# Which engine issues which transfer: patch writes on GpSimd's queue, maxima on SyncE between the patch loads

## The chip, the cores and the metric

One core of one Trainium2 chip runs the whole kernel. The metric is the time of one execution in device microseconds (us). Most executions of one kernel agree within 0.3%; all runs compared here are undisturbed (fast) ones. Five engines run in parallel, each with its own in-order queue: TensorE (PE; its weight loads are PEld), VectorE (DVE), ScalarE (ACT), GpSimd (POOL) and SyncE (SP), which only issues transfers here.

## The reference

Each of two layers replaces a 3x3 convolution by a soft lookup. Every channel's nine-pixel patch is compared with 16 centroids, a softmax over the 16 distances makes weights, and the weights pick from a table.

```python
def amm_conv3x3(x, centroids, w_sub, stride=1):          # x: (16, 256, 28, 28), centroids: (256, 16, 9)
    patches = conv_general_dilated_patches(x, (3, 3), (stride, stride), 'SAME')
    p = patches.reshape(B, C, s, Ho * Wo).transpose(0, 3, 1, 2)
    d = sum(p * p)[..., None] - 2.0 * einsum('bncs,cks->bnck', p, centroids) + sum(centroids * centroids)
    attn = softmax(-d, axis=-1)
    lut = einsum('cks,cso->cko', centroids, w_sub)
    out = einsum('bnck,cko->bno', attn, lut)
    return out.transpose(0, 2, 1).reshape(B, -1, Ho, Wo)
# per image: group norm -> amm (layer 0) -> batch norm, relu -> amm (layer 1) -> batch norm
#            -> squeeze-excite gate -> relu(. + its input) -> + x
```

## The kernel before

The work is cut into 32 stages (16 images, two layers), and each stage into 16 slots of 5 to 7 us (two tiles of 384 and 400 pixels, 8 groups of channels each). Stages of the two layers alternate. In a slot TensorE multiplies patches with centroids (the logits, L563), ScalarE exponentiates (L621), TensorE multiplies the exponentials with the centroids (the numerators, L631), VectorE transposes these (nt, L643) and takes reciprocals (rc, L649), GpSimd scales (k, L659, and small sums, L671), VectorE transposes back (q) and TensorE accumulates outputs (L695).

Three kinds of transfer feed this. **Patch writes** (L468): the image and two shifted copies of it are written to a patch buffer in device memory, 12 writes for an image and layer, during the stage before it is used. **Patch loads** (L550): SyncE reads four pieces of that buffer for each slot, three slots ahead. **Maxima**: for two of the eight groups of channels of layer 1 the largest logit is found six slots ahead, and is moved to the rows of the patch tile by way of device memory: `mt` (VectorE) to `dm` (L602), then `dm` to `pt` (L608).

```python
def to_pat(l, i, pat, px=0, n=HW):                     # patch write; L468 is the issue
    dx, k, h = STEPS[i]
    ...
    nc.scalar.dma_start(view(pat, ...), bass.AP(v.tensor, ...))      # [cut]

def patches(u, tile):                                  # patch loads of one slot
    ...
    for i in range(4):
        nc.sync.dma_start(pt[32 * i : 32 * i + ROWS, :, :n], view(u["pat"], ...))   # L550 [cut]

def m_turn(u):                                         # VectorE, L595
    mt = small.tile([P, 4, 32], F32, name="mt")
    nc.vector.transpose(mt..., u["mx"]...)             # [cut]

def m_out(u):
    d = drot.tile([4 * 256, 32], F32, tag="dm", name="dm")
    for p0, n in ((0, P), (P, 96)):
        nc.scalar.dma_start(view(d, ...), u["mt"][:n])               # L602 [cut]
    u["dm"] = d

def m_in(u):
    for j in range(NCH):
        nc.scalar.dma_start(u["pt"][MROW + j :: 32, :, :n], view(u["dm"], ...))     # L608 [cut]

# the order of work within one slot
LOGITS, EXP, LOOK_A, NUM, TURN, SMALL, LOOK_B, MAX, LOOK_C, TURN_BACK, LOAD, REST = range(12)
...
    a = s - self.lb                                    # six slots ahead
    at(a, MAX, a_logits, u)
    ...
    at(a + 2, TURN_BACK, m_turn, u)
    at(a + 3, TURN, m_out, u)
    at(a + 4, TURN, m_in, u)
```

## Time and profile before

| | before |
|---|---|
| time, median of 2 (range) | 3105.42 us (3103.16 to 3107.68) |
| span of the profiled run, mean granted clock | 3103.0 us, 0.972 |
| TensorE busy, idle | 2966.8 us (96%), 136 us |
| the 13 layer-0 stages between 396 and 2711 us, mean | 96.7 us |
| the layer-1 stages (14), mean | 88.3 us |
| first logits, first numerators start | 45.7 us, 54.8 us |

The stage times are the distances between the first numerator matmuls of successive stages in the timeline. Time at half clock counts as busy, so the 136 us of idle time aren't all that can be won.

The lines themselves are in the prediction below. A waits line such as `SPq L550 <- DMA pat<-side: 650.6, 180, 14.0` reads: instructions of line 550 on SyncE's queue were held until a transfer pat<-side landed, 650.6 us in total, 180 times, at most 14.0 us. The `q` marks the queue, which for SyncE is all there is.

### The profile page before, as it was taken

How to read it: one execution, taken by the hardware profiler on the slowest of the kernel's cores; microseconds unless marked ns; L12 is line 12 of the kernel's file. 1: busy time of each engine (PE TensorE's matmuls, PEld its weight loads, DVE VectorE, ACT ScalarE, POOL GpSimd, SP SyncE). 2: the span in 40 equal slices, each digit the busy share in tenths (PEclk: the TensorE clock that was granted, in tenths of full speed). 3: DMA queues.
4: the chain of work that ended last, by engine and by line, in shares of the span. 5: the costliest groups of instructions: out<-in, count | busy, mean ns of one | idle time of the engine just before them, and what ended most of it. 6: DMA issues, size and time to landing. Idle time of an engine off the chain costs nothing.

```text
span 3103.0 us, 94273 instructions
## 1 busy us (share of the span) xinstructions
PE 2966.8 (96%) x39834; PEld 1165.8 (38%) x39834; DVE 2254.3 (73%) x2760; ACT 1094.8 (35%) x1605; POOL 1506.4 (49%) x2163
## 2 busy tenths in 40 slices
PE   4998999999999999999999999999999999999997
PEld 3432333333333333333333333333333433334333
DVE  3464777777777777777777787777777777777785
ACT  2331342433434233342433334243343423333332
POOL 2352454555545455464545545455453545546444
PEclk8998999999999999999999999999999999999998
DMA  7866777767757676675767767676775767664552
GB/s 204 215 148 133 202 201 188 190 163 190 187 148 188 148 202 169 182 183 146 192 158 199 182 165 184 157 194 156 192 187 144 193 148 202 171 170 114 146 136 58
DMA packets 339391, 530.25 MB, mean 171 GB/s; under 512 B 94240, under 2 KB 265488, under 8 KB 338960
## 3 DMA queue, kind: packets, MB, share of 16 engines
q10 hardware_dynamic: 151488, 244.45, 31.5%
q1 hardware_dynamic: 180560, 241.14, 30.6%
q0 software_dynamic: 6912, 38.54, 4.2%
q8 instruction: 316, 5.18, 0.7%
q14 instruction: 115, 0.94, 0.1%
HBM read 269.96 MB, written 254.05 MB: 169 GB/s over the span
## 4 chain that ended last, share of the span: by engine, by line
PE 76%; DMA 10%; DVE 5%; POOL 3%; issue 2%; ACT 2%; ACTq 1%; SPq 0%; POOLq 0%; DVEq 0%
PE acc L695 45%; PE pair L631 15%; PE pair L563 15%; DMA pt<-pat 6%; DMA pat<-side 3%; DVE nt L643 2%; POOL k L659 1%; DVE rc L649 1%; ACT e L621 1%; DVE q L677 1%; POOL total L671 1%; DMA pat<-im 1%; ACTq L468 1%; PE pair L324 1%; DVE gn_st L417 0%
## 5 line engine op out<-in xcount | busy, mean ns | idle before, releaser
L695 PE MATMUL acc<-q,ws 128*128 128x384 f32 (+1 forms) x4096 | 1662.5, 525 | 5.3 <-ACT y L717 5.3
L659 POOL TENSOR_TENSOR k<-nt,rc 128x832 f32<-128x832 f32 (+1 forms) x512 | 804.8, 1572 | 1538.5 <-DVE rc L649 1527.1
L643 DVE STREAM_TRANSPOSE nt<-pair 128x832 f32<-128x832 f32 (+1 forms) x1024 | 977.4, 993 | 765.3 <-PE pair L631 640.7
L621 ACT ACTIVATE e<-pair 128x800 f32<-128x800 f32 (+1 forms) x1024 | 787.3, 821 | 1499.7 <-PE pair L563 1308.7
L695 PEld LDWEIGHTS acc<-q,ws 128*128 128x128 f32 x4096 | 705.1, 191 | 922.5 <-issue 610.0
L563 PE MATMUL pair<-pt,wd 19*32 19x384 f32 (+2 forms) x18432 | 626.5, 509 | 60.5 <-DMA pt<-pat 58.6
L631 PE MATMUL pair<-e,cw 32*32 32x384 f32 (+1 forms) x16384 | 585.9, 507 | 14.5 <-ACT e L621 13.3
L677 DVE STREAM_TRANSPOSE q<-k 128x832 f32<-128x832 f32 (+1 forms) x512 | 489.2, 956 | 0.8 <-POOL k L659 0.8
L649 DVE RECIPROCAL rc<-nt 128x104 f32<-128x104 f32 (+1 forms) x512 | 398.6, 779 | 17.6
L563 PEld LDWEIGHTS pair<-pt,wd 19*32 19x32 f32 (+1 forms) x18432 | 149.3, 103 | 440.6 <-issue 265.6
L631 PEld LDWEIGHTS pair<-e,cw 32*32 32x32 f32 x16384 | 167.2, 104 | 360.5 <-ACT e L621 317.9
L665 POOL TENSOR_TENSOR tail<-nt,rc 128x104 f32<-128x104 f32 (+1 forms) x512 | 245.1, 479 | 0.0
L695 PE MATMUL acc<-qt,ws 128*128 128x400 f32 (+1 forms) x512 | 218.8, 509 | 0.0
L671 POOL TENSOR_TENSOR total<-total,nt 128x96 f32<-128x96 f32 (+1 forms) x448 | 200.3, 447 | 0.0
L671 POOL TENSOR_TENSOR total<-total,rc 128x96 f32<-128x96 f32 (+1 forms) x448 | 179.1, 400 | 0.0
L695 PEld LDWEIGHTS acc<-qt,ws 128*128 128x128 f32 x512 | 91.0, 190 | 100.8 <-issue 51.3
L587 DVE TENSOR_REDUCE mx<-z 128x48 f32<-128x768 f32 (+1 forms) x128 | 120.8, 944 | 0.0
L582 DVE STREAM_TRANSPOSE z<-pair 128x768 f32<-128x768 f32 (+1 forms) x128 | 119.4, 971 | 1.8 <-PE pair L563 1.8
L707 ACT ACTIVATE im<-acc,bnsh,bnsc 128x384 f32<-128x384 f32 (+1 forms) x64 | 43.4, 678 | 137.0 <-PE acc L695 135.2
L717 ACT ACTIVATE y<-acc,bnsh,bnsc 128x384 f32<-128x384 f32 (+1 forms) x64 | 43.4, 679 | 88.7 <-PE acc L695 79.5
L525 DVE SCALAR_TENSOR_TENSOR y<-xt,gn_rstd,y 128x392 f32<-128x392 f32 x64 | 71.2, 1116 | 1.2 <-ACT y L519 1.2
L533 POOL TENSOR_TENSOR y<-y,xt 128x392 f32<-128x392 f32 x64 | 64.8, 1015 | 11.0 <-ACT y L529 11.0
(104 smaller groups left out, 620.7 us busy)
## 6 DMA issues: line engine op xcount, KB each, us to landing
pat<-side ACTq DMA_DIRECT2D x232, 588.0 KB
pt<-pat SPq DMA_DIRECT2D x1024, 112.5 KB
pt<-pat SPq DMA_DIRECT2D x1024, 108.0 KB
pat<-im ACTq DMA_DIRECT2D x116, 588.0 KB
xt<-in_x POOLq DMA_DIRECT2D x32, 784.0 KB, 8.7
out_dram<-y POOLq DMA_DIRECT2D x16, 784.0 KB, 6.4
pat<-side ACTq DMA_DIRECT2D x24, 300.0 KB
pat<-side ACTq DMA_DIRECT2D x24, 288.0 KB
```

The lines of the kernel that those rows point to most:

```text
L563: nc.tensor.matmul(ps[t // 2][c : c + 32, t % 2, :n], lhsT=wd[l][32 * i : 32 * i + rows, 4 * u["m"] + t, :], rhs=u["pt"][32 * i : 32 * i + ...
L582: nc.vector.transpose(z[:, : 64 * nb].rearrange("p (t m) -> p t m", t=2), ps[:, :, : 32 * nb])
L587: nc.vector.tensor_reduce(u["mx"][:, 2 * v : 2 * v + 2].rearrange("p t (j b) -> p t b j", j=2)[:, :, :nb], u["z"].pop(0)[:, : 64 * nb].rea ...
L621: nc.scalar.activation(e[:, :, :n], ps[:, :, :n], AF.Exp, scale=2.0)
L631: nc.tensor.matmul(u["nm"][t // 2][32 * i : 32 * i + 32, t % 2, :n], lhsT=cw[l][c : c + 32, 4 * u["m"] + t, :], rhs=es[t // 2][c : c + 32, ...
L643: nc.vector.transpose(nt[:, :nb, 2 * v : 2 * v + 2].rearrange("p b t r -> p t b r"), ps[:, :, : 32 * nb].rearrange("p t (b r) -> p t b r", ...
L649: nc.vector.reciprocal(rc[:, : 8 * nb], u["nt"][:, :, SUM])
L659: nc.gpsimd.tensor_tensor(q[:, :nb].rearrange("p b (a s) -> p (b a) s", s=8), nt[:, :, :8], rc.unsqueeze(2).to_broadcast([P, 8 * nb, 8]), ...
L665: nc.gpsimd.tensor_tensor(tails[key][:, :nb, 8 * (m % 4) : 8 * (m % 4) + 8], nt[:, :, 8].rearrange("p (b a) -> p b a", a=8), rc.rearrange( ...
L671: nc.gpsimd.tensor_add(t[:, : 8 * nb], t[:, : 8 * nb], v)
L677: nc.vector.transpose(q[:, :, : 32 * nb].rearrange("p h (b r) -> p h b r", r=32), u.pop("k")[:, :nb].rearrange("p b (h r) -> p h b r", h=2),)
L695: nc.tensor.matmul(accs[key][:, :n], lhsT=ws[l][:, 2 * m + h if h < 2 else 2 * NQ + m // 4, o * P : (o + 1) * P], rhs=u["q"][h][:, :n], st ...
```

## The change

The intent: ScalarE, which has exponentials to do, loses both kinds of transfer that it issues all through the run. The patch writes go to GpSimd, the maxima to SyncE, and in a slot SyncE's loads and then the maxima now come right behind the logits.

```diff
@@ to_pat
-        nc.scalar.dma_start(
+        nc.gpsimd.dma_start(
@@ m_out
-            nc.scalar.dma_start(view(d, 32 * p0, ...), u["mt"][:n])
+            nc.sync.dma_start(view(d, 32 * p0, ...), u["mt"][:n])
@@ m_in
-            nc.scalar.dma_start(
+            nc.sync.dma_start(
@@ the order within a slot
-    LOGITS, EXP, LOOK_A, NUM, TURN, SMALL, LOOK_B, MAX, LOOK_C, TURN_BACK, LOAD, REST = range(12)
+    LOGITS, LOAD, MOVE, EXP, LOOK_A, NUM, TURN, SMALL, LOOK_B, MAX, LOOK_C, TURN_BACK, REST = range(13)
-                        at(a + 3, TURN, m_out, u)
-                        at(a + 4, TURN, m_in, u)
+                        at(a + 3, MOVE, m_out, u)
+                        at(a + 4, MOVE, m_in, u)
```

## The prediction

> **What bounds the kernel now.** I read the page first (busy shares, then clock), then TensorE's waits, then SyncE's own waits, then the stretches around one stall. The first two parts of the page:
>
> ```profile
> PE 2966.8 (96%) x39834; PEld 1165.8 (38%) x39834; DVE 2254.3 (73%) x2760; ACT 1094.8 (35%) x1605; POOL 1506.4 (49%) x2163
> ...
> PEclk8998999999999999999999999999999999999998
> DMA  7866777767757676675767767676775767664552
> ```
>
> (The DMA row is the 40 slices' busy share.) TensorE is busy 96% of 3103 us and nothing else comes near, so only its idle time and its slow time can be won. The idle time is 136 us; TensorE's waits say what ends it (us in total, times, longest):
>
> ```profile
> PE pair L563 <- DMA pt<-pat: 58.6, 39, 4.9
> PE pair L423 <- DVE gn_mv L418: 14.9, 2, 12.3
> PE pair L631 <- ACT e L621: 13.3, 23, 4.5
> ```
>
> The largest is matmuls waiting for the patch loads (SyncE's pt<-pat); only 13.3 us wait for ScalarE. So why are loads late, with a lead of three slots (512 slots, 6 us each)? SyncE's own waits over the run:
>
> ```profile
> SPq L550 <- DMA pat<-side: 650.6, 180, 14.0
> SPq L550 <- DMA pat<-im: 404.4, 63, 15.1
> SPq L550 <- DMA pt<-pat: 378.1, 491, 4.6
> SPq L550 <- DMA dm<-mt: 304.6, 55, 21.4
> ```
>
> The patch loads wait 1360 us for transfers that ScalarE issues (patch writes pat<-side and pat<-im, maxima dm<-mt). Nearly all of it isn't data: the patch buffers were written a stage earlier. The built program gives the DMAs of SyncE and ScalarE together eight completion semaphores, taken in turn in program order, and each DMA waits for the earlier one on its semaphore. So a load waits for the write eight DMAs before it, and that write waits in ScalarE's queue behind exponentials and behind the wait for dm to land. One such place in stretches (us; busy time of PE, PEld, DVE, ACT, POOL; clock; DMA share; GB/s):
>
> ```profile
> 1020.00:1034.00 14.00, 14.00 (x183) 5.14 (x182) 11.92 (x16) 3.13 (x4) 7.72 (x11) 1.00 0.74 195
> 1034.00:1039.00 5.00, 1.43 (x4) 0.31 (x4) 1.74 (x2) 0.00 (x0) 2.00 (x4) 0.96 0.80 214
> 1039.00:1045.00 6.00, 6.00 (x40) 1.67 (x41) 0.00 (x0) 1.56 (x2) 0.00 (x0) 0.50 0.62 139
> ```
>
> From 1025.2 to 1033.5 us SyncE waits once, 8.3 us, for a pat<-side that ScalarE issued at 1025.90. ScalarE's timeline there:
>
> ```profile
> 1024.78 1.08 ACTq L602 DMA_DIRECT2D dm<-mt  x2
> 1025.90 0.61 ACTq L468 DMA_DIRECT2D pat<-side  x1
> ...
> 1032.11 1.17 ACTq L608 DMA_DIRECT2D pt<-dm  x2
> ```
>
> The load misses its slot, TensorE stands 3.6 us, and then runs 6 us at clock 0.50: the stall costs twice. What it costs in all is seen from equal stretches, each with the 512 numerator matmuls of one stage (16 slots):
>
> ```profile
> 952.40:1049.90 97.50, 93.25 (x1245) 35.75 (x1244) 69.06 (x82) 37.04 (x56) 51.04 (x77) 0.96 0.71 177
> 2711.20:2798.80 87.60, 87.60 (x1235) 34.50 (x1234) 68.13 (x81) 30.43 (x43) 41.21 (x58) 1.00 0.64 164
> 2798.80:2885.50 86.70, 86.70 (x1244) 34.55 (x1243) 69.24 (x82) 32.37 (x49) 49.55 (x70) 1.00 0.48 113
> ```
>
> The first is a layer-0 stage with the stall, the second a layer-1 stage, the third a layer-0 stage with no patch writes beside it and no stall. Cutting the timeline the same way, the 13 layer-0 stages between 396 and 2711 us take 93.8 to 98.5 us, mean 96.7; the layer-1 stages 87.5 to 90.5.
>
> **What the Trainium skill says.** (1) "DMA: Bandwidth & Descriptors", section "Issuing engines are not separate DMA queues": all issuers' transfers interleave on the same 16 engines, and another issuer saves only sequencer time. The trace agrees on the engines (share 0.74 with both queues active), so I expect no bandwidth from the move; but it doesn't speak of the coupling through shared semaphores that I found above. (2) "TensorE: Matmul & The Clock Gate", Part 1, "What's actually happening": an idle window of some 3.4 us brings the clock to half, a busy one restores it. The trace agrees: 0.50 for 6 us after the 5 us hole. (3) "Perfetto Trace Analysis", section "DMA Instruction — SWDGE (GPSIMD)": what is recorded of a GpSimd DMA is descriptor generation by its cores, up to the last core. So I take the recorded 756 ns (out<-y) and 812 ns (xt<-in) medians as time taken from GpSimd. (4) "SBUF — State Buffer", "SBUF: two separate sides": a VectorE operation in a two-port mode keeps GpSimd from writing descriptors. No sign of it here: the 32 xt issues took 747 to 872 ns beside a VectorE busy 73%.
>
> **The change part by part.**
> ScalarE loses 420 patch writes of about 0.60 us (582 to 610 median), 128 dm of 0.45 and 128 pt<-dm of 0.567: 252 + 58 + 73 = 383 us of its sequencer, and the 118.4 us that it stood before an exponential until dm had landed. Beside TensorE's work almost all of that was hidden: worth 10 us of the 13.3 at most.
> GpSimd gains 420 issues of about 0.78 us (my choice between 756 and 812): 328 us, 1506 + 328 = 1834 us, 59%. In a slot: k 1.57, tail 0.48, totals 0.85 make 2.9 us, plus 0.78 is 3.7 of 6 us. It still has room. VectorE's nt waits 103 us already for GpSimd's totals (two nt buffers), all catching up after stalls, so a GpSimd that is late by a slot would be felt.
> SyncE gains 256 issues of about 0.5 us, 128 us, and 64 waits for dm to land (7.3 us in the timeline above: 1024.78 to 1032.11). It has loads three slots ahead, 18 us, so 7 us fits.
> The coupling goes: in the changed program the hardware semaphores belong to SyncE alone and GpSimd's DMAs use the eight software ones. Loads wait for real data or earlier loads.
> Gains: 13 stages x (96.7 - 87.6) = 118 us, of which I take 90%, 106; the layer-1 stages' small stalls, 10 us in all, half: 5; the near stall at 2926.8 us, 6; the stretch from 180 to 305 us, which takes 126 us where a clean stage takes 88 and where loads and weight moves on SyncE wait for patch writes: 10 of 38, as true dependences stay there.
> Losses: at the start GpSimd now issues 12 patch writes before sq (L389, at 16.4 us before). 12 x 0.78 = 9.4 us, and writes 9 to 12 wait for the semaphores of 1 to 4; sq moves to about 27 us, and with it VectorE's sorting, which releases TensorE at 33.5 us. Part was slack behind loads: 9 us lost. Where patch writes are close before their loads (image 0 and image 15 of layer 1), GpSimd's turn in a slot comes some 6 us after ScalarE's, since scaling waits for numerators and VectorE: 3 us.
> Sum: 106 + 5 + 6 + 10 - 9 - 3 = 115 us; 3105 - 115 = 2990.
>
> **Rivals.**
> A, GpSimd becomes the gate: its in-order queue stands at a patch write (waiting for a semaphore or for side), scaling is late, nt buffers aren't free, TensorE's ring fills. For: 103 us of such waits now, and in slots 0 to 3 there are four writes each. Against: 59% load. If each stage lost 3 us by it: 32 x 3 = 96, hence about 3085, the same.
> B, the wait moves: SyncE stands for dm to land and the loads behind it are late. For: longest wait on dm 21.4 us. Against: that was ScalarE's queue; now dm goes out when the maxima are ready, with three slots before use. Half the gain lost would be 3045.
> C, loads were late from DMA contention. For: share 0.80 in the hole. Against: SyncE issued nothing for 8.3 us before it, and the stretch before has 0.74 at full speed. If C, 3090.
> D, everything goes, also 38 us of the start: 2950.
>
> **Range and chances.** I weigh: main line 70%, A or B in part 20%, C or worse 10%. **2990 us**, range 2950 to 3060. Faster by over 2% means under 3043: 0.82; within 2%: 0.15; slower: 0.03.
>
> **What would show it.** Right: SyncE's waits name no pat<-side except at a stage's first load; PE waiting for pt<-pat falls from 58.6 to under 20 us; layer-0 stages take 87 to 89 us; clock dips between 300 and 2700 us vanish; GpSimd's pat issues take 0.7 to 0.9 us; first logits come near 54 us instead of 45.7. Wrong: issues over 1.2 us, or VectorE's nt waiting for GpSimd in hundreds of us (A); pt<-pat waits released by dm landings (B); holes with loads issued in time (C).

## More of the kernel before

The program names no completion semaphores. Whoever builds it hands them out to the transfers and adds the waits.

## The result, and the profile after

The changed kernel takes **2973.64 us** (median of 2, 2970.91 to 2976.36), the kernel before 3105.42. The ratio is 0.9576, with a 95% interval of 0.9527 to 0.9624. A ratio here is always the mean time of one kernel's fast runs over the mean time of the other's fast runs of the same rounds, so it isn't quite the ratio of the medians quoted.

The page of the kernel after, busy time, granted clock and DMA share:

```profile
PE 2871.6 (97%) x39834; PEld 1145.4 (39%) x39834; DVE 2252.7 (76%) x2760; ACT 1092.7 (37%) x1605; POOL 1768.5 (60%) x2583
...
PEclk8999999999999999999999999999999999999998
...
DMA  6877777767767676776767667676776767674641
```

TensorE executes the same 39834 matmuls in 95.2 us less busy time. Its idle time falls from 136 to 98 us. So 38 us of the gain are in the holes themselves, and more is in what follows them: summed over the trace, the time lost to halved clock (the missing share of the clock times its duration) is 88.4 us before and 32.2 us after, 56 us less. The rest of the 95 us isn't taken apart. All 12 dips between 300 and 2700 us are gone. The DMA row hardly moves, so there is no sign that the transfers became cheaper.

TensorE's waits after (total us, times, longest):

```profile
PE pair L423 <- DVE gn_mv L418: 20.6, 14, 12.3
PE pair L396 <- POOL sq L389: 12.9, 1, 12.9
PE pair L631 <- ACT e L621: 10.6, 20, 6.4
PE acc L695 <- ACT y L717: 9.7, 1, 9.7
...
PE pair L563 <- DMA pt<-pat: 3.3, 7, 0.7
```

The wait that led the list before, logits for patch loads, fell from 58.6 us to 3.3. Three lines have grown: the wait for `sq` at the start (3.0 us before), the many short waits for group-norm statistics (`gn_mv`, 14.9 before) and one wait near the end for the last layer's output `y` (5.3 before). All are looked at below. SyncE's own waits after:

```profile
SPq L550 <- PE pair L563: 580.6, 361, 5.7
SPq L602 <- DVE mt L595: 547.5, 62, 15.2
SPq L550 <- DMA pt<-pat: 245.4, 327, 3.0
...
SPq L550 <- DMA pat<-side: 59.0, 10, 9.9
```

The loads now wait mostly for TensorE to release a patch buffer, which is the wait that one wants, or for earlier loads. Waits for patch writes fell from 1055 us (pat<-side and pat<-im) to 59. Note the second line: SyncE stands 547.5 us until VectorE has the maxima ready, up to 15.2 us at a time, and yet loads arrive in time, because three slots are more than 15 us.

Two successive stages of the kernel after, layer 0 and then layer 1 (us; busy time of PE, PEld, DVE, ACT, POOL; clock; DMA share; GB/s):

```profile
1254.00:1342.30 88.30, 87.71 (x1248) 34.63 (x1248) 69.31 (x82) 37.08 (x56) 59.25 (x89) 1.00 0.72 187
1342.30:1430.10 87.80, 87.45 (x1237) 34.65 (x1236) 70.57 (x87) 30.46 (x44) 49.23 (x71) 1.00 0.68 180
```

A layer-0 stage takes 88.3 us at full clock where the one shown in the prediction took 97.5 at 0.96. Slot by slot, most of that is in the fifteenth slot: 14.8 us on average in the thirteen layer-0 stages before, 7.46 in each of them after.

Where the time went, from the starts of the stages in both traces (us, negative is a gain):

| part | before | after | difference | predicted |
|---|---|---|---|---|
| first numerators start | 54.8 | 60.8 | +6.0 | +9 |
| first stage | 124.9 | 117.0 | -7.9 | 0 |
| second stage (from 180 us) | 125.8 | 103.6 | -22.2 | -10 |
| 13 layer-0 stages | 1257.8 | 1149.2 | -108.6 | -106 |
| 14 layer-1 stages | 1235.4 | 1235.6 | +0.2 | -5 |
| stage from 2799 us | 86.7 | 86.4 | -0.3 | 0 |
| stage from 2886 us | 97.9 | 89.1 | -8.8 | -6 + 3 |
| last stage and end | 119.6 | 127.5 | +7.9 | 0 |
| span | 3103.0 | 2969.2 | -133.8 | -115 |

### The profile page after: what moved, and what is told of

The parts are those of the page before. It is cut to its first block, busy times and chain, and to the rows that moved or that the text cites. A ratio compares the mean times of both kernels' runs of the same rounds, so it can differ in the third digit from the quotient of the medians.

```text
span 2969.2 us, 94838 instructions
## 1 busy us (share of the span) xinstructions
PE 2871.6 (97%) x39834; PEld 1145.4 (39%) x39834; DVE 2252.7 (76%) x2760; ACT 1092.7 (37%) x1605; POOL 1768.5 (60%) x2583
## 4 chain that ended last, share of the span: by engine, by line
PE 79%; DMA 7%; DVE 6%; POOL 4%; issue 2%; ACT 2%; SPq 0%; ACTq 0%; DVEq 0%; POOLq 0%
PE acc L695 47%; PE pair L631 16%; PE pair L563 14%; DMA xt<-in_x 4%; DVE nt L643 2%; POOL k L659 2%; DVE rc L649 1%; DVE gn_st L417 1%; POOL total L671 1%; DMA pt<-pat 1%; ACT e L621 1%; DMA ws<-dws 1%; PE pair L309 0%; PE pair L324 0%; DVE q L677 0%
## 5 line engine op out<-in xcount | busy, mean ns | idle before, releaser
L695 PE MATMUL acc<-q,ws 128*128 128x384 f32 (+1 forms) x4096 | 1641.0, 519 | 9.7 <-ACT y L717 9.7
L695 PEld LDWEIGHTS acc<-q,ws 128*128 128x128 f32 x4096 | 696.9, 189 | 907.7 <-issue 577.2
L631 PE MATMUL pair<-e,cw 32*32 32x384 f32 (+1 forms) x16384 | 580.3, 502 | 11.9 <-ACT e L621 10.6
L563 PE MATMUL pair<-pt,wd 19*32 19x384 f32 (+2 forms) x18432 | 561.0, 500 | 5.9 <-DMA pt<-pat 3.3
L563 PEld LDWEIGHTS pair<-pt,wd 19*32 19x32 f32 (+1 forms) x18432 | 138.4, 103 | 340.1 <-issue 265.5
L468 POOL DMA_DIRECT2D pat<-side x280 | 186.6, 667 | 1.1 <-DMA pat<-im 0.7
L468 POOL DMA_DIRECT2D pat<-im x140 | 94.0, 672 | 3.5 <-ACT im L447 3.5
```

The costliest lines, as they stand in the source:

```text
L468: nc.gpsimd.dma_start(view(pat, (ROWS * p0 + 9 * k + 3 * dx) * HW + px, [[ROWS * HW, m], [HW, 3], [1, n]]), bass.AP(v.tensor, v.offset, [l ...
L563: nc.tensor.matmul(ps[t // 2][c : c + 32, t % 2, :n], lhsT=wd[l][32 * i : 32 * i + rows, 4 * u["m"] + t, :], rhs=u["pt"][32 * i : 32 * i + ...
L631: nc.tensor.matmul(u["nm"][t // 2][32 * i : 32 * i + 32, t % 2, :n], lhsT=cw[l][c : c + 32, 4 * u["m"] + t, :], rhs=es[t // 2][c : c + 32, ...
L695: nc.tensor.matmul(accs[key][:, :n], lhsT=ws[l][:, 2 * m + h if h < 2 else 2 * NQ + m // 4, o * P : (o + 1) * P], rhs=u["q"][h][:, :n], st ...
```

## The experiments

Twelve kernels were run, each in three rounds against the kernel before on the same chip, whose median there lay between 3107 and 3110 us. All gave correct results. Where an edit adds lines, line numbers in that kernel's trace are up to two higher.

| run | kernel | median us (range) | ratio to before [95%] |
|---|---|---|---|
| e1_pat_only | before + only patch writes to GpSimd | 3110.73 (3107.61 to 3111.84) | 1.0013 [0.9992, 1.0035] |
| e2_max_only | before + only maxima to SyncE, with the new order | 3033.74 (3024.67 to 3035.87) | 0.9757 [0.9730, 0.9783] |
| e3_order_only | before + loads early in the slot (built the same program, see below) | 3109.40 (3104.28 to 3114.92) | 1.0014 [0.9991, 1.0037] |
| e10_old_order | after, in the old order | 2974.66 (2970.66 to 2978.24) | 0.9568 [0.9537, 0.9599] |
| e4_ticks | after + tiny unrelated transfers on ScalarE | 3035.80 (3030.02 to 3043.10) | 0.9765 [0.9739, 0.9790] |
| e9_max_on_act | after, maxima back on ScalarE | 3330.48 (3328.10 to 3335.38) | 1.0715 [1.0682, 1.0748] |
| e7_pool_busy | after + more work on GpSimd | 2984.57 (2984.05 to 2986.70) | 0.9599 [0.9570, 0.9628] |
| e11_all_gpsimd | before, patch writes and maxima to GpSimd, old order | 3147.74 (3144.10 to 3155.68) | 1.0121 [1.0096, 1.0145] |
| e12_gpsimd_early | after, maxima on GpSimd, new order | 2973.85 (2972.79 to 2979.95) | 0.9572 [0.9547, 0.9597] |
| e5_sq_first | after + squares ahead of the first writes | 2964.37 (2962.18 to 2967.47) | 0.9536 [0.9507, 0.9565] |
| e6_xt_early | after + input images one slot earlier | 2963.25 (2962.48 to 2965.42) | 0.9524 [0.9508, 0.9540] |
| e8_best | after + four repairs | 2942.73 (2937.89 to 2947.80) | 0.9465 [0.9447, 0.9482] |

**The theory**: transfers of SyncE and of ScalarE share eight completion semaphores, and one that reuses a semaphore waits for the transfer that used it before. Loads were late because they stood behind ScalarE's issues in this way, and the change ends it by leaving ScalarE without regular issues. **The rivals**: the place in the slot (new order) does it; the load on the DMA engines does it; or GpSimd's or SyncE's new issues cost what was won.

### e1: the patch writes alone

```diff
@@ before, to_pat
-        nc.scalar.dma_start(
+        nc.gpsimd.dma_start(
```

> Only the patch writes go to GpSimd; the moves of the maxima stay with ScalarE and the order of the slot is as before. Theory (loads are late because they share completion semaphores with ScalarE's patch writes): nearly all of the gain, 2975 to 3005 us; SyncE's loads wait no more for pat, only for dm and pt<-dm; layer-0 stages 88 to 90 us. Rival 1 (the maxima, through ScalarE's wait for dm to land, make the loads late): 3050 us or more. Rival 2 (both parts are needed): some 3030 to 3060.

Measured: 3110.73 us, no gain at all. The theory's 2975 to 3005 us failed, because it took the waits for the maxima to be harmless. The first rival's 3050 us or more came true, but e2 below will speak against the maxima as the only cause. SyncE's waits, then TensorE's, over the whole run:

```profile
SPq L550 <- DMA dm<-mt: 837.3, 80, 24.0
...
SPq L550 <- DMA pat<-side: 57.4, 13, 12.4
```

```profile
PE pair L563 <- DMA pt<-pat: 43.0, 42, 3.4
```

The loads no longer wait for patch writes (57.4 us), but they wait 837.3 us for the maxima instead, up to 24.0 us, and TensorE still waits 43.0 us for them. The two layer-0 stages from 1132 and 1318 us take 96.2 and 96.8 us, with the fifteenth slot at 15.5 and 15.8. One such place: between 1000 and 1032 us SyncE's queue has

```profile
SPq L550 <- DMA dm<-mt: 24.6, 2, 23.0
```

and ScalarE's timeline of the same kernel has the issues that it waits for:

```profile
1016.36 1.56 ACT L621 ACTIVATE e<-pair 128x800 f32<-128x800 f32 x2 [3.50 <-PE pair L563]
1019.15 1.92 ACTq L602 DMA_DIRECT2D dm<-mt  x2
...
1025.78 2.54 ACTq L608 DMA_DIRECT2D pt<-dm  x2
```

The first dm goes out at 1019.15, as soon as VectorE has the maxima ready (1019.12), and lands at 1023.75. The load is issued at 1023.81, after 23.0 us of waiting for it, which is more than the 18 us of three slots. A load of patches has no use for maxima. In the trace the load waits on the very semaphore that this dm counts, and then counts on it itself.

The semaphore numbers, which the trace keeps for every transfer, show the same over the whole run. Of the 1360 us that loads wait for ScalarE's transfers in the kernel before, 1339 are waits on the semaphore that the load itself uses next; so are all 837.3 us here. The 2835 transfers of the two queues before make one strict turn through eight semaphores (354 or 355 transfers each). In this turn the late load of the prediction (issued at 1033.51) comes eight places after the patch write of 1025.90. But the turn isn't the written order: the first dm of that stage takes its turn behind 766 loads, where the program writes 776 ahead of it.

### e2: the maxima alone

```diff
@@ before, m_out and m_in
-            nc.scalar.dma_start(
+            nc.sync.dma_start(
@@ and the new order within a slot, as in the change
```

> Only the moves of the maxima go to SyncE, with the new places of loads and moves in the slot; the patch writes stay with ScalarE. Theory: loads still share semaphores with the patch writes, so little is won: 3060 to 3110 us, SyncE's waits for pat still several hundred us. Rival 1 (the maxima are the cause): 2980 to 3000. Worse than before is possible if SyncE now also stands for dm behind ScalarE's writes.

Measured: 3033.74 us, 72 us less than the kernel before (74 in its own rounds) and 60 more than the kernel after. That lies between the theory's 3060 to 3110 and the rival's 2980 to 3000, so neither forecast held. SyncE's waits:

```profile
SPq L550 <- DMA pat<-side: 558.0, 180, 13.7
SPq L550 <- DMA pat<-im: 410.8, 62, 17.2
```

The patch writes, left on ScalarE, still hold the loads 969 us, and the fifteenth slot of two layer-0 stages checked takes 9.8 and 11.8 us. So the two parts don't add: patch writes alone give 0, maxima alone 72, and patch writes after the maxima 60 more. Two streams hold the same loads. With one gone the other holds them nearly as long or, being the one that comes last, just as long.

### e3 and e10: the order in the slot

```diff
@@ e3: before + only
-    ... LOOK_C, TURN_BACK, LOAD, REST = range(12)
+    LOGITS, LOAD, EXP, LOOK_A, ... TURN_BACK, REST = range(12)
@@ e10: after, with the list and the places (TURN) of before
```

> Only the place of the loads in the slot's program order moves (ahead of the exponentials instead of near the end); every DMA keeps its engine. Theory: the loads' own waits are unchanged, so 3095 to 3110 us, the same. Rival (the order of issue is the cause): under 3050.

> The changed kernel with one part undone: patch writes on GpSimd and maxima on SyncE, but the order of the slot as before, so that a slot's dm and pt<-dm are issued ahead of its loads. If sharing semaphores with ScalarE is the cause, the order adds little: 2970 to 2995 us. If the place between the loads is needed (SyncE then stands for the maxima in front of a load that is needed soon): 3000 to 3060 us, with loads late behind dm.

Measured: 3109.40 us (1.0014, interval around 1) and 2974.66 us (0.9568, against 0.9576 for the kernel after). But e3 tests nothing. Its edit swaps loads and moves in 64 places of the written order, and yet its trace has the same instructions as the kernel before, with the same semaphores, and the same order of transfers in every queue: the built program didn't change. e10 is a test: SyncE's transfers do stand in another order there. So the order is worth nothing measurable with the new assignment of the queues. With the maxima on ScalarE it is worth much, and in the wrong direction (e9 below).

### e4: the coupling by itself

The tick is a transfer of 64 bytes from a constant into a tile that nobody reads. It shares no data and no buffer with a load. It stands where the patch writes stood in ScalarE's queue.

```diff
@@ after
+    ticks = [const.tile([1, 16], F32, name=f"tick{i}") for i in range(12)]
@@ to_pat, ahead of the write
+        nc.scalar.dma_start(ticks[i], consts[0:1, 0:16])
```

> The changed kernel, and beside each of the 420 GpSimd patch writes ScalarE issues a DMA of 64 bytes to a tile that nobody reads, at the place where its patch write stood. It carries no data and almost no traffic, but takes its turn in the semaphores that the loads use. Theory: SyncE's loads wait for these ticks again, for tens to hundreds of us in all; [...]only part of the stalls comes back: 2985 to 3040 us. Rival (the loads were late because of the writes' data in ScalarE's queue or on the DMA engines, not because of the shared semaphores): 2970 to 2980 us, the same as the changed kernel, with no wait of loads for ticks.

Measured: 3035.80 us, 62 us more than the kernel after. SyncE's waits:

```profile
SPq L552 <- DMA tick<-in_consts: 784.4, 211, 15.8
```

Loads of patches wait 784.4 us for transfers that they have nothing to do with, and two layer-0 stages checked take 91.3 and 94.2 us instead of 88.3. 420 ticks of 64 bytes are 27 KB beside the 530 MB that the page reports for the whole run, so neither data nor bandwidth can be the reason. Nor is it the time that ScalarE spends on them: a tick takes its queue 0.23 us (median), and TensorE waits 11.2 us for exponentials, 10.6 in the kernel after. All 784.4 us are waits on the semaphore that the load itself uses next. This shows the shared semaphores at work. It also comes within about 2 us of e2 (3033.74 us), where real patch writes stood in the same places; the thirteen layer-0 stages together take 1205 us here, 1199 in e2 and 1149 in the kernel after.

### e9: the maxima back on ScalarE

```diff
@@ after, m_out and m_in, at the new early place
-            nc.sync.dma_start(
+            nc.scalar.dma_start(
```

> The changed kernel with one part undone: the maxima are issued by ScalarE again (at the new places MOVE), the patch writes stay with GpSimd and the loads early in the slot. The run with the patch writes alone moved won nothing: its loads waited 837 us for dm. Theory A (the engine matters: any DMA of ScalarE that shares the loads' semaphores and is issued late holds them): 3050 to 3110 us, with hundreds of us of loads waiting for dm and 5 or so fewer loads issued before a stage's first dm than the program places there. Theory B (the order in the slot was what was missing there): 2970 to 2990 us.

Measured: 3330.48 us, far outside both forecasts. This run doesn't isolate what it was made for. It differs from e1 by the order in the slot alone, and is 220 us slower. At the new place the moves stand ahead of the slot's exponentials in ScalarE's queue, so a second loss comes in: TensorE's waits are led by

```profile
PE pair L631 <- ACT e L621: 233.3, 85, 6.4
```

which was 10.6 us. The loads again wait 948.9 us for dm, but TensorE waits only 9.8 us for loads. So most of this loss isn't the coupling. The cleaner test of the same question is e1.

### e7: is GpSimd close to being the bound?

```diff
@@ after
+    busy = const.tile([P, 704], F32, name="busy")
@@ to_pat, ahead of the write
+        nc.gpsimd.memset(busy, 0.0)
```

> The changed kernel with a GpSimd memset of 128x704 (some 0.66 us, from 0.96 us for 128x1024) ahead of each of the 420 patch writes: GpSimd's cost of the move doubled, some 280 us more of its time. If GpSimd is off the path (theory): 2970 to 2985 us, GpSimd near 69% busy. If its queue already sets VectorE's pace in part (rival A of the prediction): 3000 us or more, with VectorE's nt waiting for GpSimd in hundreds of us.

Measured: 2984.57 us, 11 us more than the kernel after, for 259 us more work on GpSimd (1768.5 to 2027.6 us, 68%). The stages in the middle stay at 88.3 us. The loss lies at the start (the third stage starts 10 us later than in the kernel after), where the first writes and their new companions stand ahead of `sq`. The kernel's own line for it:

```profile
PE pair L397 <- POOL sq L390: 18.9, 1, 18.9
```

(12.9 in the kernel after). First numerators start at 65.3 us instead of 60.8. Away from the start GpSimd has room for at least 0.6 us more beside each patch write.

### e11 and e12: patch writes and maxima on GpSimd, late and early

If only the coupling counted, any queue apart from ScalarE's and SyncE's would do for the maxima. e11 is the kernel before with patch writes and maxima on GpSimd, in the old order.

```diff
@@ e11: before, to_pat, m_out and m_in
-        nc.scalar.dma_start(
+        nc.gpsimd.dma_start(
@@ e12: after, m_out and m_in
-            nc.sync.dma_start(
+            nc.gpsimd.dma_start(
```

> The kernel before with both kinds of ScalarE's DMAs moved to GpSimd: patch writes and maxima; order of the slot as before, SyncE keeps only its loads. Theory (loads are free once no DMA of another, later engine shares their semaphores; SyncE as the issuer of the maxima isn't needed): 2975 to 3005 us, layer-0 stages 88 to 90 us, no load waiting for dm. Rival (the maxima have to be on the loads' own queue): 3030 or more. GpSimd pays 256 more issues, those of dm with 512 and 384 runs of 128 bytes probably over 1 us each, and stands for dm to land: some ten us.

Measured: 3147.74 us, 1.2% slower than the kernel before. The expectation of a gain failed. The coupling itself is gone, as SyncE's waits of e11 show:

```profile
SPq L550 <- PE pair L563: 1704.5, 470, 8.3
```

There is no line for dm left among the loads' waits. But TensorE has a new one:

```profile
PE pair L563 <- DMA pt<-dm: 144.7, 62, 4.6
```

GpSimd's timeline of e11 around such a place:

```profile
1475.22 1.52 POOL L602 DMA_DIRECT2D dm<-mt  x2
...
1477.88 1.62 POOL L659 TENSOR_TENSOR k<-nt,rc 128x832 f32<-128x832 f32 x1 [0.51 <-DVE rc L649]
...
1480.63 1.21 POOL L608 DMA_DIRECT2D pt<-dm  x2
```

The maxima go out only behind the slot's scaling, because TURN stands behind the numerators in the written order and k itself waits for VectorE's reciprocals. Then the way back stands behind the next slot's k too. It is issued at 1480.63, is over at 1481.84 and lands 4.1 us after issue (median); TensorE starts those logits at 1485.40, 3.59 us late. That suggested the place in an in-order queue as the cause, and e12 tests it: the same moves on GpSimd, but at the new place, ahead of k.

> The changed kernel with the moves of the maxima issued by GpSimd instead of SyncE, but at the new, early place in the slot. With the moves on GpSimd at the old, late place (3147.7 us) the loads no longer waited for maxima, but the first slots of a unit waited 144.7 us (62 times) for pt<-dm, whose issue stood behind the slot's k in GpSimd's queue. Theory (the place in an in-order queue, not the engine, made that loss): here the issues stand ahead of the slot's k, about 3 us earlier, TensorE's wait for pt<-dm falls under 50 us and the time is 2970 to 3020 us. Rival (GpSimd itself is too slow for 256 more issues of 0.6 to 0.75 us, 171 us, and VectorE waits for its sums): the time stays above 3080 us and VectorE's wait for GpSimd's total rises well over the 97.6 us seen there.

Measured: **2973.85 us**, the time of the kernel after. TensorE's waits and GpSimd's timeline of e12:

```profile
PE pair L563 <- DMA pt<-dm: 17.0, 19, 1.9
```

```profile
1373.02 1.51 POOL L602 DMA_DIRECT2D dm<-mt  x2 [0.23 <-DVE mt L595]
1375.32 1.52 POOL L659 TENSOR_TENSOR k<-nt,rc 128x768 f32<-128x768 f32 x1 [0.80 <-DVE rc L649]
...
1379.32 1.22 POOL L608 DMA_DIRECT2D pt<-dm  x2 [0.74 <-DMA dm<-mt]
1380.72 1.51 POOL L659 TENSOR_TENSOR k<-nt,rc 128x768 f32<-128x768 f32 x1 [0.19 <-DVE rc L649]
```

Now each move stands ahead of its slot's k, and the wait falls from 144.7 to 17.0 us. Between e11 and e12 lie 174 us, made by the written order alone; GpSimd is busy 1935.5 us in one and 1937.9 in the other. The rival (GpSimd too slow for 256 more issues) falls: VectorE's nt waits 97.6 us for its sums in e11 and 90.3 in e12. So order does nothing where the issuing queue has nothing else to do (e10) and a lot where it has: on GpSimd the early place wins 174 us (e11, e12), on ScalarE it loses 220 (e1, e9).

One thing more: SyncE stood 547.5 us for VectorE's maxima in the kernel after, and doesn't in e12, where the time is the same. That alone doesn't show that the standing is free, because e12 has a loss of its own (its thirteen layer-0 stages take 1161 us instead of 1149). But in the kernel after, TensorE waits only 3.3 us for loads and 0.5 for pt<-dm in all, so the standing can hardly cost more.

### e5, e6 and e8: what the change left over

```diff
@@ e5: after, at the start
+    square_codes(0)                # ahead of the first 12 to_pat
     for i, (dx, k, h) in enumerate(STEPS):
@@ e6: after
-            plan.at(n0 - 2, REST, load_x, b, x[b])
+            plan.at(n0 - 3, REST, load_x, b, x[b])
@@ e8: both, and
+    bn_setup()                     # too, ahead of the first 12 to_pat
-    hpool = ctx.enter_context(tc.tile_pool(name="hpool", bufs=1))
+    hpool = ctx.enter_context(tc.tile_pool(name="hpool", bufs=2))
```

> The changed kernel, with the squares of the codes (L389 on GpSimd) issued ahead of the first twelve patch writes. In the changed kernel TensorE waits 12.9 us for them and the first numerators come 6 us later than before. If that delay is what the start lost: squares at 16 to 18 us, first numerators near 55 us, 2964 to 2970 us, 4 to 9 us under the changed kernel. If the patch loads set the start anyway: no change.

> The changed kernel with the load of the next image (xt) issued one slot earlier. VectorE's statistics wait 23 us for it there (14 times), which they didn't before the change; in layer-1 stages the slot in question is 0.1 to 1.3 us longer than it was. If that wait reaches TensorE: 5 to 10 us under the changed kernel, 2964 to 2970. If not: 2973.

Measured: e5 2964.37 us, 9.3 less than the kernel after; e6 2963.25 us, 10.4 less. Both are some 0.3%, as much as executions of one kernel differ, and their intervals overlap with that of the kernel after. For e6 the stages confirm it: the fourteen layer-1 stages take 1225 us instead of 1236. For e5 they don't: first numerators start at 59.0 us, not near 55 as expected, and without this edit at 59.3 in e6 and e12. In e5 the wait for `sq` falls from 12.9 to 3.0 us, but the next GpSimd work behind the writes, the batch-norm constants, now holds TensorE once:

```profile
PE pair L261 <- DVE scratch L260: 12.8, 1, 12.8
```

For e6, the line in VectorE's waits of the kernel *after* that it removes (it isn't among the largest of the kernel before):

```profile
DVE gn_st L417 <- DMA xt<-in_x: 23.0, 14, 2.5
```

The input image now arrives as its group-norm statistics are due. VectorE stands up to 2.5 us, and in the fifteenth slot of layer-1 stages TensorE is late by up to 1.3 us. One slot more of lead removes the line, and TensorE's waits for `gn_mv` fall from 20.6 to 15.2 us.

> The version that the runs point to: the changed kernel, with squares and the batch norm's scales ahead of the first patch writes (two thirds of the start's loss), xt a slot earlier, and a second buffer for y, so that the last image's first evacuation doesn't wait 13 us for the store of the one before (TensorE waited 9.7 us there). Expected 2974 - 10 - 5 - 5 to 9, so 2945 to 2958 us.

Measured: 2942.73 us, 0.9465 of the kernel before and 31 us under the kernel after: the fastest of all. First logits start at 50.7 us (57.0 after, 45.7 before), first numerators at 54.5 (60.8 after, 54.8 before), every layer-1 stage from the third to the twenty-ninth takes 87.6 us or less, and the last stage takes 82.4 us up to its last slot instead of 93.9. The last comes with the second buffer for the last layer's outputs. In the kernel after, TensorE waited there 9.7 us for ScalarE, which in turn waited for the store of the image before; that wait isn't among the largest of e8. Those 31 us aren't taken apart beyond e5 and e6.

## Why the prediction was right, and where it was not

**The time and its main step held.** Predicted 2990 us and a range of 2950 to 3060; measured 2973.64. The step that carries it, the thirteen layer-0 stages, was sized at 106 us and gave 108.6. Their stages were to take 87 to 89 us and take 88.3 to 89.2. The clock dips between 300 and 2700 us vanish as said, and the logits' wait for loads falls under 20 us, to 3.3. That the transfers of SyncE and ScalarE are coupled through eight semaphores taken in turn is now shown by itself (e4, and the semaphore numbers of the traces). In the kernel after, SyncE has them to itself but for eight transfers of ScalarE.

**A step that failed: how the semaphores are handed out.** The prediction said "taken in turn in program order". The turn holds, the program order doesn't: a dm takes its turn behind 766 loads where 776 are written ahead of it, and e3 changes the written order without changing one semaphore. How the order of the turn is found is not shown.

**A step that was too narrow: the cause of the stall.** The prediction read the stall from one pat<-side, and "a load waits for the write eight DMAs before it". Someone who believed that would have moved the patch writes alone, and e1 shows 0 us for it. The dm of the same place holds the same loads up to 24.0 us. Only both together set them free. The prediction was saved by the change moving both.

**Mis-sized terms.** The second stage, on SyncE crowded with weight loads, gave 22.2 us where 10 of 38 were expected; why "true dependences stay there" held less back isn't shown. The stage from 2886 us gave 8.8 for the 3 expected. The first stage gave 7.9 us that were not on the list. The layer-1 stages gave nothing for the 5 expected: their old stalls went and the new wait for input images took their place (e6 shows that this wait is worth 10.4 us). The last stage and the end lost 7.9 us where 0 stood: its first output waits for the store of the image before, which holds TensorE 9.7 us instead of 5.3, and e8, with a second buffer, takes 11.5 us off this part. Why the wait grew isn't shown. The start was sized at 9 us for the first numerators and lost 6.0; first logits came at 57.0 us, not near 54. The mechanism, GpSimd's `sq` and batch-norm work behind twelve patch writes, is shown by e5 and e8 together: with `sq` alone ahead (e5) the batch-norm constants hold TensorE instead and the start hardly moves, with both ahead (e8) first numerators are back at 54.5 us. All of this together is the 19 us between a sum of 115 and a span that fell by 134.

**GpSimd's issue.** Predicted 0.78 us from the larger transfers; measured, line L468 of the kernel after (ns, min/median/max):

```profile
L468 POOL DMA_DIRECT2D pat<-side x280: 621/672/684, 20.5 to 2836.0; - x140
L468 POOL DMA_DIRECT2D pat<-im x140: 620/675/751, 17.8 to 2808.7; - x140
```

That is 281 us instead of 328, with medians under the 0.7 to 0.9 us of the prediction's list, and GpSimd's busy time is 1768.5 us instead of 1834. (Two slips change nothing: rival B's 3045 should be 3048, and of the "5 us hole" TensorE stood 3.6.)

**The rivals.** A (GpSimd becomes the gate) falls by e7. B (the wait moves to SyncE) is half true: SyncE does stand 547.5 us, but TensorE then waits only 3.3 us for loads. C (DMA contention) falls by e4, where 27 KB bring back 62 us, and by the kernel after, which moves the same 530 MB without the stalls. D (everything goes, 2950) was nearly reached: 24 us are missing.

**Why a reuse has to wait** is told by the Trainium skill, "DMA: Bandwidth & Descriptors", section "Why a DMA increments its semaphore by 16 and not by 1": two transfers in flight on one semaphore can't be told apart, hence "One semaphore per in-flight slot, not one per stream." The built program keeps that rule by waiting before each reuse (that this is its reason isn't shown), and the trace shows the price: two queues are tied together (784.4 us of waits in e4).

## What to carry to other kernels

When a load waits for a transfer with which it shares no data, suspect a shared completion semaphore, and test it with a transfer of a few bytes from the suspected queue before moving real ones. Two streams that hold the same waiter must both go: moving one may show nothing (here 0 us), moving both 132. And when a transfer moves into a queue that also computes, test its place: the same moves gained 174 us by going ahead of GpSimd's scaling, which waits for others, and lost 220 us by going ahead of ScalarE's exponentials, for which TensorE waits.

Before a run without effect is called a result, look whether the edit reached the built program: that of e3 didn't.

## What the Trainium skill lacked or had wrong

- **"DMA: Bandwidth & Descriptors"**, section "Issuing engines are not separate DMA queues", has another issuer save only the sequencer's time. As to bandwidth that agrees here (DMA share 0.71 in a layer-0 stage before, 0.72 after), but it's not all that an issuer decides. 420 transfers of 64 bytes on ScalarE cost 62 us (e4), because SyncE and ScalarE share completion semaphores in this program; the page doesn't mention it.
- **No page that I read** gives the cost of a transfer's place in an in-order computing queue: 3147.7 us behind GpSimd's scaling, 2973.9 ahead of it (e11, e12); 3110.7 us late in ScalarE's slot, 3330.5 early (e1, e9).
- **"TensorE: Matmul & The Clock Gate"**, Part 1, "What's actually happening", gives "≥1" busy window of about 3.4 us for the return to full clock, and one isn't what to reckon with. Of the 12 dips of the kernel before between 300 and 2700 us, 11 last 6.83 us at 0.5 and one 10.24, two and three times as long; at half clock 6.83 us lose 3.4, about as much again as the hole of 3.6 us before it.
- **"SBUF — State Buffer"**, section "SBUF: two separate sides", warns of VectorE keeping GpSimd from its descriptors. No run shows it: GpSimd's issue of a patch write (up to 588 KB) took 0.62 to 0.75 us in the kernel after, beside a VectorE busy 76%. Which of VectorE's operations here are of the kind that the page means was not looked into.
